# A mixture-of-experts kernel: the first expert product turned round, with the block's matrix as the stationary operand

## Chip, cores and metric

The kernel runs on one core of one Trainium2 chip. The metric is the time of one execution on the device, in microseconds (us), as the median of several runs; the core's engines are called PE (matrix multiplication, with its weight loads shown apart as PEld), DVE (vector), ACT (activation), POOL (general purpose) and SP (which here only issues transfers). All data are fp32, and all products are fp32.

## The reference

Eight sequences of 512 tokens with 256 features go through four steps, each added to the residual: attention with 16 heads and a linear position bias; a mixture of experts; attention with 8 heads and rotary positions; the same mixture of experts again. Both attentions are causal. The mixture of experts, cut to what matters here:

```python
h = x * rsqrt(mean(x * x) + eps) * norm_w          # after a layer norm
logits = h @ gate_w.T + gate_b                     # 8 experts
vals, idx = top_k(logits, 2)
wts = softmax(vals)
t1 = einsum('td,efd->tef', h, mlp1_w) + mlp1_b     # 256 -> 2 x 256
glu = minimum(t1[..., ::2], 7.0)
lin = clip(t1[..., 1::2], -7.0, 7.0)
act = glu * sigmoid(1.702 * glu) * (lin + 1.0)
y = einsum('tei,edi->ted', act, mlp2_w) + mlp2_b   # 256 -> 256
out = x + sum over the two chosen experts of wts * y
```

## The kernel before

**Stages.** An attention stage walks over 8 sequences and 8 head groups; between its steps it puts pieces of other work, among them the norm, gate, choice and count of the experts for the sequence before. When a group of sequences (the first six, then the last two) has been counted, its tokens are sorted by expert into blocks of 128 rows, each block with rows of one expert only: 55 blocks for the first group, 23 for the second, so 78 in each expert stage and 156 in the kernel. Then the expert stage (`run`, lines 960 to 975) works through the blocks. Twice over, this gives: attention, experts, attention, experts.

**One block.** Six steps, each with its own lag behind the block counter `n`, so that several blocks are under way at once:

- `gather` (line 862), four blocks ahead: POOL fetches the block's rows from DRAM by an indirect transfer, four blocks to a tile.
- `turn_rows` (874): PE turns the rows (two transposes into `gtp`), ACT copies them to `hT` (line 882).
- `first` (895), one block later: PE multiplies, with `hT` stationary and the expert's 512 columns moving (line 902), into `hp`, tokens on partitions. DVE adds the bias row (912), caps the gate (913), clips the linear half (916) and multiplies twice (917, 918); ACT computes the sigmoid between them (914). The results lie in one tile `u`.
- `turn_act` (921), three blocks after that: PE turns the result (`atp`, line 927) and ACT copies it to `aT` (929).
- `second` (932): PE multiplies with `aT` stationary (937), DVE adds the second bias (947), POOL scatters the rows to DRAM (948).

All experts' matrices stay in SBUF in one tile `we`. Which expert a block has is known only at run time: `at_block` (885) reads a number into a register of the engine that needs it, and the operand's address is that register plus a constant. The biases lie in a tile `be`, copied to all partitions, so that a block's bias is a row of 512 or 256 columns.

**Order.** PE runs in the order in which the program is written; a scheduler orders the other engines' instructions by its own estimates. [...] Within one iteration of `run`:

```python
at(n + LEAD, self.gather)
at(n - 4, self.turn_act)
at(n, self.turn_rows)
at(n - 1, self.first)
at(n - 4, self.second)
for piece in aside.get(n, ()):
    piece()
```

The `aside` pieces are the rest of the last sequence (about the first eleven iterations), the sorting of the second group (iterations 14, 17 and 20), and, from iteration 60 on, the collecting of finished results: `collect` reads rows back and `add` (line 1018) adds them on DVE to the residual, weighted. In the second expert stage this covers all sequences of the first group, two tiles every other iteration.

**Buffers.** PSUM tiles all come from one ring of eight (`ps`). Of the SBUF rings, `kb` (eight buffers) holds `hT` and `aT`, `S` (four) holds `u`, `V` (two) the results of four blocks, `qk` (two) the gathered rows of four blocks.

**Set-up.** `spread_biases` (192) runs in batch 0: it turns the first bias by PE, sends it to DRAM and reads it back onto all partitions, with 18 transfers in all. `fold_norm` (213) multiplies the norm weights into the gate matrix and the first expert matrices and adds one to the linear half of the bias, on POOL.

Of the kernel before, what the change touches and what calls it, by code (L numbers as in the profile page):

```python
# [35 lines left out]
F32 = mybir.dt.float32  # L36
# [3 lines left out]
ALU = mybir.AluOpType  # L40
# [4 lines left out]
P = 128  # L45
# [30 lines left out]
ROWS = 4  # L76

W_COLS = NC * 2 * FI + FI // P * D
B_COLS = 2 * FI + D

@with_exitstack
def layers(
# [64 lines left out]
    be_sb = const.tile([P, NE * B_COLS], F32, tag="be", name="be")  # L147
    for e in range(NE):
        o = e * W_COLS
        mid = o + NC * 2 * FI  # L150
# [39 lines left out]
    nc.vector.memset(ones, 1.0)  # L190

    def spread_biases():


        b1_sb = work.tile([P, NE * 4], F32, tag="kb", bufs=8, name="b1_p")
        nc.sync.dma_start(out=b1_sb, in_=b1.rearrange("p e m -> p (e m)"))
        b1_ps = ps.tile([NE * 4, P], F32, tag="ps", bufs=8, name="b1_ps")
        nc.tensor.transpose(b1_ps, b1_sb, ident)
        b1_rows = work.tile([NE * 4, P], F32, tag="kb", bufs=8, name="b1_rows")
        nc.vector.tensor_copy(b1_rows, b1_ps)  # L200
        b1_flat = dram.tile([NE * 4, P], F32, tag="b1_flat", name="b1_flat")
        nc.sync.dma_start(out=b1_flat, in_=b1_rows)
        for e in range(NE):
            o = e * B_COLS
            nc.sync.dma_start(
                out=be_sb[:, o : o + 2 * FI],
                in_=b1_flat[4 * e : 4 * e + 4, :].rearrange("m k -> (m k)").partition_broadcast(P),
            )
            nc.sync.dma_start(
                out=be_sb[:, o + 2 * FI : o + B_COLS], in_=b2[e].partition_broadcast(P)  # L210
            )

    def fold_norm():


        for c in range(NC):
            nc.gpsimd.tensor_scalar(
                gates_sb[:, c, 0:NE], gatew_sb[:, c, :], normw_sb[:, c : c + 1], 1.0, ALU.mult, ALU.mult
            )
        for e in range(NE):  # L220
            for c in range(NC):
                w = we_sb[:, e * W_COLS + c * 2 * FI : e * W_COLS + (c + 1) * 2 * FI]
                nc.gpsimd.tensor_scalar(w, w, normw_sb[:, c : c + 1], 1.0, ALU.mult, ALU.mult)
# [297 lines left out]
    class Experts:  # L521


        def __init__(self, kind):
            self.kind = kind
            self.x_mid = dram.tile([NB, T, D], F32, tag=f"x_{kind}", name=f"x_mid_{kind}")
            self.h_all = [
                dram.tile([(hi - lo) * T, D], F32, tag=f"h_{kind}_{i}", name=f"h_all_{kind}_{i}")
                for i, (lo, hi) in enumerate(GROUPS)
            ]  # L530
            self.y_all = [
                dram.tile([2 * PLANE + n * P, D], F32, tag=f"y_{kind}_{i}", name=f"y_{kind}_{i}")
                for i, n in enumerate(BLOCKS)
            ]
# [6 lines left out]
            self.rows, self.hT, self.act, self.ys, self.got = {}, {}, {}, {}, {}  # L541
            self.pairs = {}

        def open_group(self, i):
# [162 lines left out]
        def slots(self, i):  # L707
# [174 lines left out]
            nc.scalar.copy(h, tp)  # L882
            self.hT[i, j] = h

        def at_block(self, i, j, which, engine, cols):
            a = self.R[i]["where"][which]
            return nc.values_load(
                a[0:1, j : j + 1],
                engines=[engine],
                min_val=0,  # L890
                max_val=(NE - 1) * cols,
                skip_runtime_bounds_check_because="the expert's number is clipped",
            )

        def first(self, i, j):
            key = f"{self.kind}_{i}_{j}"
            h = self.hT.pop((i, j))
            wat = self.at_block(i, j, 0, mybir.EngineType.PE, W_COLS)
            bat = self.at_block(i, j, 1, mybir.EngineType.DVE, B_COLS)
            hp = ps.tile([P, 2 * FI], F32, tag="ps", bufs=8, name=f"hp_{key}")  # L900
            for c in range(NC):
                nc.tensor.matmul(  # L902
                    hp,
                    lhsT=h[:, c * P : (c + 1) * P],
                    rhs=we_sb[:, bass.DynSlice(wat + c * 2 * FI, 2 * FI)],
                    start=(c == 0),
                    stop=(c == NC - 1),
                )
            u = work.tile([P, PACKED], F32, tag="S", bufs=4, name=f"u_{key}")
            t, g, a = u[:, 0 : 2 * FI], u[:, 2 * FI : 3 * FI], u[:, 3 * FI : 4 * FI]  # L910
            s = u[:, 4 * FI : 5 * FI]
            nc.vector.tensor_tensor(t, hp, be_sb[:, bass.DynSlice(bat, 2 * FI)], ALU.add)  # L912
            nc.vector.tensor_scalar(g, t[:, 0:FI], LIMIT, 1.0, ALU.min, ALU.mult)  # L913
            nc.scalar.activation(s, g, AF.Sigmoid, scale=ALPHA)  # L914
# [4 lines left out]
            self.act[i, j] = a, wat, bat  # L919

        def turn_act(self, i, j):
            key = f"{self.kind}_{i}_{j}"
            a, wat, bat = self.act.pop((i, j))
            tp = ps.tile([P, FI], F32, tag="ps", bufs=8, name=f"atp_{key}")
            for c in range(FI // P):
                s = slice(c * P, (c + 1) * P)
                nc.tensor.transpose(tp[:, s], a[:, s], ident)  # L927
            aT = work.tile([P, FI], F32, tag="kb", bufs=8, name=f"aT_{key}")
            nc.scalar.copy(aT, tp)  # L929
            self.act[i, j] = aT, wat, bat  # L930

        def second(self, i, j):
            key = f"{self.kind}_{i}_{j}"
            aT, wat, bat = self.act.pop((i, j))
            yp = ps.tile([P, D], F32, tag="ps", bufs=8, name=f"y2_{key}")
            for c in range(FI // P):
                nc.tensor.matmul(  # L937
                    yp,
                    lhsT=aT[:, c * P : (c + 1) * P],
                    rhs=we_sb[:, bass.DynSlice(wat + NC * 2 * FI + c * D, D)],  # L940
                    start=(c == 0),
                    stop=(c == FI // P - 1),
                )
# [12 lines left out]
            tc.declare_no_dep(made.ins, group=group, reason="the rows of the slots differ")  # L956
            tc.add_to_no_dep_group(group, made.ins)
            self.writes[i].append(made.ins)

        def run(self, aside):  # L960
            blocks = [(i, j) for i, n in enumerate(BLOCKS) for j in range(n)]

            def at(n, work_on):
                if 0 <= n < len(blocks):
                    work_on(*blocks[n])

            for n in range(-LEAD, len(blocks) + 4):
# [263 lines left out]
```

## Time and profile before

| | us |
|---|---|
| median of 3 runs (lowest, highest) | 2336.13 (2334.91, 2338.15) |
| profiled execution, its own time | 2302.66 |
| its span, first to last instruction | 2300.8 |
| PE busy | 2229.6 |
| PE weight loads busy | 1452.9 |
| DVE busy | 1635.5 |
| ACT busy | 977.9 |
| POOL busy | 989.9 |
| first product, first and last start, stage one | 937.8 and 1197.7 |
| first product, first and last start, stage two | 2019.6 and 2278.9 |

The durations come from the profiled execution, which was some 33 us shorter than the median of the runs. Busy times are sums of durations. A matmul's end is modelled, and consecutive instructions of one engine overlap in the records, so a busy share is not a rate; where a rate matters it is taken from start to start. In lines of groups the columns are: line, engine, operation, output and inputs, shape, count, then busy us and mean ns of one, then the idle time of the engine just before, and what ended it.

### The profile page before, as it was taken

The page shows a single profiled execution, that of the slowest core. Times are in us where ns is not written, and L with a number is a line of the kernel's source. Part 1 is how long each engine was busy: PE and PEld are TensorE (multiplying, and loading weights), DVE is VectorE, ACT ScalarE, POOL GpSimd, SP SyncE. Part 2 cuts the span into 40 slices and gives each one's busy share as a digit, 9 for nine tenths or more (in the row PEclk, how much of TensorE's full clock was granted, in tenths as well). Part 3 has the DMA queues.
Part 4 walks back from the last instruction along what each step waited for, and adds up shares of the span by engine and source line. Part 5 has one row for each costly group of instructions (what it writes and reads, how often), then busy time and mean ns, then how long its engine had stood idle before and what let it go on. Part 6 is the DMA issues. An engine that isn't in the chain of part 4 may idle for free.

```text
span 2300.8 us, 34673 instructions
## 1 busy us (share of the span) xinstructions
PE 2229.6 (97%) x10657; PEld 1452.9 (63%) x10657; DVE 1635.5 (71%) x4926; ACT 977.9 (43%) x2828; POOL 989.9 (43%) x1374
## 2 busy tenths in 40 slices
PE   8999999999999999899999999999999999999994
PEld 5666666666666666556556666666666666665662
DVE  5566666666666777687877677776867678778787
ACT  4555555555555555323234343443433433433331
POOL 5443434343433343556644333343433434445662
PEclk9999999999999999999999999999999999999997
DMA  7100000000000001222310011010101000022247
GB/s 241 38 28 1 28 1 29 1 28 1 28 1 28 6 28 70 99 79 88 103 52 15 10 37 33 15 46 5 42 10 37 14 33 28 19 78 81 88 156 231
DMA packets 80005, 112.54 MB, mean 49 GB/s; under 512 B 10288, under 2 KB 64720, under 8 KB 79824
## 3 DMA queue, kind: packets, MB, share of 16 engines
q1 hardware_dynamic: 63760, 68.37, 9.0%
q0 software_dynamic: 14976, 40.91, 5.7%
q8 instruction: 89, 1.46, 0.3%
q10 hardware_dynamic: 1088, 1.05, 0.2%
q14 instruction: 92, 0.75, 0.1%
HBM read 68.86 MB, written 41.44 MB: 48 GB/s over the span
## 4 chain that ended last, share of the span: by engine, by line
PE 88%; DVE 7%; issue 2%; POOL 2%; ACT 1%; DMA 1%; DVEq 0%; ACTq 0%; POOLq 0%; SPq 0%
PE pp_a L317 9%; PE pp_b L317 9%; PE hp_f L902 9%; PE op_a L454 6%; PE sp_a L375 6%; PE tp_a L427 6%; PE sp_b L375 6%; PE op_b L454 5%; PE yp_b L472 5%; PE yp_a L472 5%; PE vp_a L298 5%; PE vp_b L298 5%; PE y_f L937 5%; PE tp_b L427 3%; PE atp_f L927 1%
## 5 line engine op out<-in xcount | busy, mean ns | idle before, releaser
L397 ACT ACTIVATE S_a<-S_a,nm_a 128x512 f32<-128x512 f32 (+3 forms) x512 | 280.3, 549 | 306.6 <-DVE nm_a L387 306.5
L330 POOL TENSOR_TENSOR qk_b<-qk_b,rot_b 128x512 f32<-128x512 f32 x128 | 162.8, 1272 | 457.0 <-DVE qk_b L329 446.8
L902 PE MATMUL hp_f<-we,hT_f 128*128 x624 | 294.4, 594 | 0.8 <-ACT hT_f L882 0.8
L356 POOL TENSOR_SCALAR ali_a<-alibi 128x512 f32<-128x512 f32 x128 | 79.4, 620 | 451.0 <-DVE nm_a L387 442.5
L397 ACT ACTIVATE S_b<-S_b,nm_b 128x512 f32<-128x512 f32 (+3 forms) x256 | 142.8, 558 | 235.3 <-DVE nm_b L387 233.8
L387 DVE CUSTOM_DVE_ANT_0 S_a<-sp_a,ali_a 128x512 f32<-128x512 f32 (+3 forms) x512 | 215.9, 486 | 30.7 <-PE sp_a L375 30.5
L412 POOL TENSOR_SCALAR S_a<-S_a,sum_a 128x384 f32<-128x384 f32 (+2 forms) x384 | 205.5, 551 | 34.7 <-DVE sum_a L408 26.2
L948 POOL DMA_INDIRECT y_f<-y_f,row_f x156 | 155.5, 997 | 131.6 <-DVE y_f L947 100.4
L867 POOL DMA_INDIRECT g_f<-h_all_f,token_f x156 | 152.1, 975 | 99.9 <-PE gtp_f L880 58.0
L914 ACT ACTIVATE u_f<-u_f 128x256 f32<-128x256 f32 x156 | 65.1, 417 | 305.0 <-DVE u_f L913 304.8
L937 PEld LDWEIGHTS y_f<-we,aT_f 128*128 128x128 f32 x624 | 117.2, 191 | 110.7 <-issue 53.3
L937 PE MATMUL y_f<-we,aT_f 128*128 x624 | 164.8, 387 | 21.6 <-ACT aT_f L929 21.6
L387 DVE CUSTOM_DVE_ANT_0 S_b<-sp_b,mask 128x512 f32<-128x512 f32 (+3 forms) x256 | 119.1, 484 | 90.5 <-PE sp_b L375 90.5
L375 PE MATMUL sp_b<-qk_b 128*128 128x512 f32 (+3 forms) x512 | 171.9, 438 | 5.0 <-POOL qk_b L330 5.0
L427 PE MATMUL tp_a<-ident,S_a 128*128 128x128 f32 x1280 | 165.3, 276 | 1.1 <-DVE O_a L462 0.6
L427 PEld LDWEIGHTS tp_a<-ident,S_a 128*128 128x128 f32 x1280 | 141.1, 141 | 31.9 <-issue 22.8
L454 PE MATMUL op_a<-PT_a,V_a 128*64 128x384 f32 (+3 forms) x1024 | 154.2, 439 | 3.3 <-ACT PT_a L437 2.2
L912 DVE TENSOR_TENSOR u_f<-hp_f,be 128x512 f32<-128x512 f32 x156 | 107.8, 691 | 68.8 <-PE hp_f L902 61.0
L375 PE MATMUL sp_a<-qk_a 64*128 64x512 f32 (+3 forms) x1024 | 155.5, 443 | 0.9 <-DVE qk_a L334 0.9
L902 PEld LDWEIGHTS hp_f<-we,hT_f 128*128 128x128 f32 x624 | 106.8, 191 | 76.0 <-issue 74.8
L437 ACT COPY PT_a<-tp_a 128x512 f32<-128x512 f32 (+1 forms) x320 | 138.6, 495 | 29.4 <-PE tp_a L427 29.4
L454 PE MATMUL op_b<-PT_b,V_b 128*128 128x512 f32 (+3 forms) x512 | 148.6, 433 | 0.0
(184 smaller groups left out, 4505.6 us busy)
## 6 DMA issues: line engine op xcount, KB each, us to landing
h_all_f<-hn_f SPq DMA_DIRECT2D x64, 128.0 KB, 1.7
xm_f<-x_mid_f SPq DMA_DIRECT2D x16, 512.0 KB, 4.1
yg_f<-y_f SPq DMA_DIRECT2D x64, 128.0 KB, 2.2
yg_f<-y_f SPq DMA_DIRECT2D x28, 256.0 KB, 4.0
x<-x_in_dram SPq DMA_DIRECT2D x8, 512.0 KB, 4.1
we<-w_dram SPq DMA_DIRECT2D x8, 512.0 KB, 7.1
x_mid_f<-x SPq DMA_DIRECT2D x8, 512.0 KB, 2.9
x_mid_f<-xm_f SPq DMA_DIRECT2D x8, 512.0 KB, 3.0
```

Of the source, the lines that this page charges most:

```text
L298: nc.tensor.matmul(vp[:, k, :], lhsT=self.xT[b][:, c, t * P : (t + 1) * P], rhs=wv[:, c, q * 2 * P : (q + 1) * 2 * P], start=(c == 0), sto ...
L317: nc.tensor.matmul(pp, lhsT=w[:, c, g * P : (g + 1) * P], rhs=self.xT[b][:, c, :], start=(c == 0), stop=(c == NC - 1),)
L330: nc.gpsimd.tensor_tensor(qk[:, j, :], qk[:, j, :], rot, ALU.add)
L375: nc.tensor.matmul(sp[i][:, at[it] : at[it] + w], lhsT=qk[r, 0, it * P : (it + 1) * P], rhs=qk[r, 1, 0:w], start=True, stop=True,)
L387: nc.vector.tensor_tensor_reduce(out=s, in0=sp[i][:, at[it] : at[it] + w], in1=add[i][:, T - w : T], scale=scale, scalar=float(np.finfo(np ...
L397: nc.scalar.activation(s, s, AF.Exp, bias=nm[:, it : it + 1], scale=-1.0, accum_out=sums[:, it : it + 1],)
L412: eng.tensor_scalar(s, s, sums[:, it : it + 1], 1.0, ALU.mult, ALU.mult)
L427: nc.tensor.transpose(tp[:, o : o + P], S[:, S_OFF[it] + jt * P : S_OFF[it] + (jt + 1) * P], ident,)
L454: nc.tensor.matmul(op[i * cols : (i + 1) * cols, jt * P : T], lhsT=v[:, jt, c0 : c0 + cols], rhs=PT[i][:, P_OFF[jt] : P_OFF[jt] + T - jt * P],
L472: nc.tensor.matmul(yp[:, 0:D], lhsT=o[:, c, t * P : (t + 1) * P], rhs=wo[:, half * HALF + c, :], start=(c == 0), stop=(c == HALF - 1),)
L902: nc.tensor.matmul(hp, lhsT=h[:, c * P : (c + 1) * P], rhs=we_sb[:, bass.DynSlice(wat + c * 2 * FI, 2 * FI)], start=(c == 0), stop=(c == N ...
L937: nc.tensor.matmul(yp, lhsT=aT[:, c * P : (c + 1) * P], rhs=we_sb[:, bass.DynSlice(wat + NC * 2 * FI + c * D, D)], start=(c == 0), stop=(c ...
```

## The change

The first product is turned round. The block's matrix is stationary and the turned rows move, so that `hp` comes out with the expert's 512 columns on partitions, in four parts of 128, and tokens along the free dimension. The activation then comes out in the layout that the second product wants, and `turn_act` with its copy is gone. Three things follow.

- The 128x1024 part of the expert's matrix is copied on ACT, from its run-time address in `we` to a tile `w1` (ring of three), two blocks ahead (`weights`). PE reads the first product's operands at fixed addresses; only the second product keeps run-time addresses on PE.
- The first bias is now one number per partition: the tile `be` holds eight numbers per expert (gate bias; the lower and the upper limit of the linear half, shifted by the bias; bias plus one; each for two halves). DVE's steps on 512 or 256 columns become steps on 128 columns, each with one or two such numbers as scalar operands at run-time addresses.
- The second bias is copied to all partitions in one transfer into a tile `b2`; the trip of the first bias through PE and DRAM is gone. DVE reads two run-time numbers per block in place of one.

The activation `a` takes a buffer of the `kb` ring. The matrices of `fold_norm` stay as they are.

```diff
-B_COLS = 2 * FI + D
+N_GATE, N_LOW, N_HIGH, N_LIN = 0, 2, 4, 6
+B_COLS = 8
...
+    b1_sb = load(const, [P, NE, 4], b1, "b1")
+    be_sb = const.tile([P, NE, B_COLS], F32, tag="be", name="be")
+    b2_sb = const.tile([P, NE * D], F32, tag="b2", name="b2")
...
     def spread_biases():
...
+        nc.sync.dma_start(
+            out=b2_sb, in_=b2.rearrange("e d -> (e d)").partition_broadcast(P)
+        )
+        lin = b1_sb[:, :, 2:4]
+        nc.gpsimd.tensor_copy(be_sb[:, :, N_GATE : N_GATE + 2], b1_sb[:, :, 0:2])
+        for at, add, by in (
+            (N_LOW, LIMIT, -1.0),
+            (N_HIGH, -LIMIT, -1.0),
+            (N_LIN, 1.0, 1.0),
+        ):
+            nc.gpsimd.tensor_scalar(be_sb[:, :, at : at + 2], lin, add, by, ALU.add, ALU.mult)
...
-            w = be_sb[:, e * B_COLS + FI : e * B_COLS + 2 * FI]
-            nc.gpsimd.tensor_scalar(w, w, 1.0, 1.0, ALU.add, ALU.mult)
...
-            for tag, cols in (("we_at", W_COLS), ("be_at", B_COLS)):
+            for tag, cols in (("we_at", W_COLS), ("be_at", B_COLS), ("b2_at", D)):
...
+        def weights(self, i, j):
+
+            wat = self.at_block(i, j, 0, mybir.EngineType.Activation, (NE - 1) * W_COLS)
+            w = work.tile([P, NC * 2 * FI], F32, tag="w1", bufs=3, name=f"w1_{self.kind}_{i}_{j}")
+            nc.scalar.copy(w, we_sb[:, bass.DynSlice(wat, NC * 2 * FI)])
+            self.w1[i, j] = w
...
         def first(self, i, j):
...
-            for c in range(NC):
-                nc.tensor.matmul(
-                    hp,
-                    lhsT=h[:, c * P : (c + 1) * P],
-                    rhs=we_sb[:, bass.DynSlice(wat + c * 2 * FI, 2 * FI)],
-                    start=(c == 0),
-                    stop=(c == NC - 1),
-                )
+            bat = self.at_block(i, j, 1, mybir.EngineType.DVE, (NE - 1) * B_COLS)
+            dat = self.at_block(i, j, 2, mybir.EngineType.DVE, (NE - 1) * D)
+            hp = ps.tile([P, 4, P], F32, tag="ps", bufs=8, name=f"hp_{key}")
+            for m in range(4):
+                for c in range(NC):
+                    o = c * 2 * FI + m * P
+                    nc.tensor.matmul(
+                        hp[:, m, :],
+                        lhsT=w[:, o : o + P],
+                        rhs=h[:, c * P : (c + 1) * P],
+                        start=(c == 0),
+                        stop=(c == NC - 1),
+                    )
...
-            nc.vector.tensor_tensor(t, hp, be_sb[:, bass.DynSlice(bat, 2 * FI)], ALU.add)
-            nc.vector.tensor_scalar(g, t[:, 0:FI], LIMIT, 1.0, ALU.min, ALU.mult)
+            for m in range(2):
+                nc.vector.tensor_scalar(
+                    half(g, m), hp[:, m, :], number(N_GATE + m), LIMIT, ALU.add, ALU.min
+                )
             nc.scalar.activation(s, g, AF.Sigmoid, scale=ALPHA)
-            lin = t[:, FI : 2 * FI]
-            nc.vector.tensor_scalar(lin, lin, 1.0 - LIMIT, 1.0 + LIMIT, ALU.max, ALU.min)
-            nc.vector.tensor_tensor(g, g, lin, ALU.mult)
+            for m in range(2):
+                nc.vector.tensor_scalar(
+                    half(lin, m),
+                    hp[:, 2 + m, :],
+                    number(N_LOW + m),
+                    number(N_HIGH + m),
+                    ALU.max,
+                    ALU.min,
+                )
+            for m in range(2):
+                nc.vector.scalar_tensor_tensor(
+                    half(g, m), half(lin, m), number(N_LIN + m), half(g, m), ALU.add, ALU.mult
+                )
             nc.vector.tensor_tensor(a, g, s, ALU.mult)
...
-        def turn_act(self, i, j):
...
-            nc.vector.tensor_tensor(y, yp, be_sb[:, bass.DynSlice(bat + 2 * FI, D)], ALU.add)
+            nc.vector.tensor_tensor(y, yp, b2_sb[:, bass.DynSlice(dat, D)], ALU.add)
...
-                at(n - 4, self.turn_act)
+                at(n + 1, self.weights)
```

`number(n)` is one column of `be` at the run-time address plus `n`; `half(t, m)` is 128 columns of a tile.

More of the change, by code (lines that the diff above doesn't have):

```diff
@@ L146, in layers @@
     we_sb = const.tile([P, NE * W_COLS], F32, tag="we", name="we")
-    be_sb = const.tile([P, NE * B_COLS], F32, tag="be", name="be")
+    b1_sb = load(const, [P, NE, 4], b1, "b1")
+    be_sb = const.tile([P, NE, B_COLS], F32, tag="be", name="be")
+    b2_sb = const.tile([P, NE * D], F32, tag="b2", name="b2")
     for e in range(NE):
@@ L192, in spread_biases @@
     def spread_biases():
[L195 to L207, printed above, removed]
-            )
-            nc.sync.dma_start(
-                out=be_sb[:, o + 2 * FI : o + B_COLS], in_=b2[e].partition_broadcast(P)
-            )
+        nc.sync.dma_start(
[9 more added lines that the diff above has]
+            nc.gpsimd.tensor_scalar(be_sb[:, :, at : at + 2], lin, add, by, ALU.add, ALU.mult)
     def fold_norm():
@@ L540, in __init__ @@
             self.hn, self.h, self.both = {}, {}, {}
-            self.rows, self.hT, self.act, self.ys, self.got = {}, {}, {}, {}, {}
+            self.rows, self.hT, self.w1, self.act, self.ys, self.got = {}, {}, {}, {}, {}, {}
             self.pairs = {}
@@ L883, in turn_rows, with at_block @@
             self.hT[i, j] = h
-        def at_block(self, i, j, which, engine, cols):
+        def at_block(self, i, j, which, engine, high):
             a = self.R[i]["where"][which]
@@ L890, in at_block @@
                 min_val=0,
-                max_val=(NE - 1) * cols,
+                max_val=high,
                 skip_runtime_bounds_check_because="the expert's number is clipped",
             )
+        def weights(self, i, j):
[3 more added lines that the diff above has]
+            self.w1[i, j] = w
         def first(self, i, j):
@@ L897, in first @@
             h = self.hT.pop((i, j))
-            wat = self.at_block(i, j, 0, mybir.EngineType.PE, W_COLS)
-            bat = self.at_block(i, j, 1, mybir.EngineType.DVE, B_COLS)
-            hp = ps.tile([P, 2 * FI], F32, tag="ps", bufs=8, name=f"hp_{key}")
-            for c in range(NC):
-                nc.tensor.matmul(
-                    hp,
-                    lhsT=h[:, c * P : (c + 1) * P],
-                    rhs=we_sb[:, bass.DynSlice(wat + c * 2 * FI, 2 * FI)],
-                    start=(c == 0),
-                    stop=(c == NC - 1),
-                )
@@ L909, in first @@
[L909 to L914, printed above, removed]
-            lin = t[:, FI : 2 * FI]
-            nc.vector.tensor_scalar(lin, lin, 1.0 - LIMIT, 1.0 + LIMIT, ALU.max, ALU.min)
@@ L917, in first @@
-            nc.vector.tensor_tensor(g, g, lin, ALU.mult)
-            nc.vector.tensor_tensor(a, g, s, ALU.mult)
-            self.act[i, j] = a, wat, bat
-        def turn_act(self, i, j):
[L922 to L930, printed above, removed]
+            w = self.w1.pop((i, j))
@@ new lines, in first, with number, half @@
+            u = work.tile([P, PACKED], F32, tag="S", bufs=4, name=f"u_{key}")
+            g, lin, s = (u[:, k * FI : (k + 1) * FI] for k in range(3))
+            a = work.tile([P, FI], F32, tag="kb", bufs=8, name=f"a_{key}")
+            flat = be_sb.rearrange("p e n -> p (e n)")
+            def number(n):
+                return flat[:, n : NE * B_COLS][:, bass.DynSlice(bat, 1)]
+            def half(t, m):
+                return t[:, m * P : (m + 1) * P]
+            for m in range(2):
+                nc.vector.tensor_scalar(
+                    half(g, m), hp[:, m, :], number(N_GATE + m), LIMIT, ALU.add, ALU.min
+                )
@@ L932, in second @@
+            nc.vector.tensor_tensor(a, g, s, ALU.mult)
+            self.act[i, j] = a, dat
         def second(self, i, j):
             key = f"{self.kind}_{i}_{j}"
-            aT, wat, bat = self.act.pop((i, j))
+            a, dat = self.act.pop((i, j))
+            wat = self.at_block(i, j, 0, mybir.EngineType.PE, (NE - 1) * W_COLS)
             yp = ps.tile([P, D], F32, tag="ps", bufs=8, name=f"y2_{key}")
             for c in range(FI // P):
+                o = NC * 2 * FI + c * D
                 nc.tensor.matmul(
@@ L938, in second @@
                     yp,
-                    lhsT=aT[:, c * P : (c + 1) * P],
-                    rhs=we_sb[:, bass.DynSlice(wat + NC * 2 * FI + c * D, D)],
+                    lhsT=a[:, c * P : (c + 1) * P],
+                    rhs=we_sb[:, o : NE * W_COLS][:, bass.DynSlice(wat, D)],
                     start=(c == 0),
```

## The prediction

> **What bounds the kernel now.** I read the engine totals first, then the table by stage, the waits of the matmul engine (PE), one block of PE's timeline, and the groups by shape.
>
> ```profile
> PE 2229.6 (97%) x10657; PEld 1452.9 (63%) x10657; DVE 1635.5 (71%) x4926; ACT 977.9 (43%) x2828; POOL 989.9 (43%) x1374
> ...
> 1025.00:1150.00 125.00, 122.94 (x485) 76.75 (x484) 101.66 (x257) 38.10 (x121) 81.00 (x83) 1.00 0.30 95
> ...
> 2107.00:2240.00 133.00, 132.77 (x529) 83.95 (x528) 108.77 (x273) 41.49 (x130) 85.36 (x88) 1.00 0.37 114
> 2240.00:2287.00 47.00, 31.49 (x120) 18.54 (x118) 39.10 (x99) 10.15 (x30) 15.98 (x16) 0.90 0.71 223
> ```
>
> The last three lines are stretches of the two expert stages (start:end, length, then busy us of PE, PEld, DVE, ACT, POOL). In the middle of both, PE is busy nearly throughout; in the last 47 us it is not, and DVE leads. PE's waits and one block:
>
> ```profile
> PE y_f L937 <- ACT aT_f L929: 21.6, 25, 2.4
> ...
> 1150.56 0.38 PE L927 MATMUL atp_f<-ident,u_f 128*128 128x128 f32 x2
> 1150.78 0.38 PE L880 MATMUL gtp_f<-ident,g_f 128*128 128x128 f32 x2
> 1151.00 1.88 PE L902 MATMUL hp_f<-we,hT_f 128*128 x4
> 1152.71 1.03 PE L937 MATMUL y_f<-we,aT_f 128*128 x4
> 1153.58 0.38 PE L927 MATMUL atp_f<-ident,u_f 128*128 128x128 f32 x2
> ```
>
> From start to start a block takes 3.02 us: 0.22 turning the activation, 0.22 turning the rows, 1.71 first product, 0.87 second, with no gap. In the trace's start times, consecutive first-product instructions lie 430 ns apart, second-product ones 216, transposes 109. A busy duration (594 ns for one of hp_f) is longer than its place in the queue, so I price PE by start to start. There are 78 blocks in each of two stages, 156 in all; almost all of the middle ones have this period. The 21.6 us of waits are the only large ones in the expert stages: the copy aT_f stands on ACT behind a sigmoid that waits for a late DVE.
>
> ```profile
> L902 PE MATMUL hp_f<-we,hT_f 128*128 x624 | 294.4, 594 | 0.8 <-ACT hT_f L882 0.8
> L912 DVE TENSOR_TENSOR u_f<-hp_f,be 128x512 f32<-128x512 f32 x156 | 107.8, 691 | 68.8 <-PE hp_f L902 61.0 <-issue 4.2 <-PE gtp_f L880 0.7
> L1018 DVE SCALAR_TENSOR_TENSOR xm_f<-yg_f,wt_f,xm_f 128x256 f32<-128x256 f32 x128 | 68.3, 546 | 9.4 <-DMA yg_f<-y_f 6.4 <-DMA out_dram<-xm_f 1.7
> L914 ACT ACTIVATE u_f<-u_f 128x256 f32<-128x256 f32 x156 | 65.1, 417 | 305.0 <-DVE u_f L913 304.8
> L454 PE MATMUL op_b<-PT_b,V_b 128*128 128x128 f32 x128 | 24.6, 274 | 0.0
> L689 PEld LDWEIGHTS cp_f<-both_f,before 128*128 128x128 f32 x32 | 6.1, 190 | 0.8
> ```
>
> Here the reader sees that DVE now waits for PE at L912 (it has room), and that ACT idles 305 us before its sigmoids.
>
> **What the Trainium skill says.** "TensorE: Matmul & The Clock Gate", LDWEIGHTS (loading the stationary operand): a load takes its columns at 1.2 per ns, 107 ns for 128. The trace agrees: in one run of L689 three loads follow each other after 109 and 113 ns. "VectorE: DVE Perf Modes", Why PSUM operands drop a tier: fp32 from PSUM runs at the single rate; L912 agrees, 608 ns of queue for 512 columns where nothing delays the next. The same page, on the errata: a fixed cost falls on every instruction, so many small tiles pay it often. The trace: L387 from start to the next takes 211, 345, 478, 612 ns for 128 to 512 columns, 77 + 1.045 per column. "ScalarE: Activation LUTs", The pipeline for one element: 0.833 ns per element; L397 on SBUF moves by 0.835.
>
> **The change, part by part** (us against the profiled execution's 2302.66, whose span is 2300.8; the median of the runs shown, 2336.13, is 33 us higher, and I carry the difference over unchanged).
>
> 1. *PE per block.* Gone: two transposes of the activation, 2 x 0.109 = 0.218. The first product goes from 4 instructions at 430 ns (1.72) to 16 of 128 columns with 16 weight loads (four column parts, two halves of the contraction, and fp32 issues each matmul twice, as 624 = 156 x 4 shows). 128-column fp32 pairs exist already: op_b (L454) and sp_b (L375) go 109 to 112 ns from start to start, weight load included. 16 x 0.110 = 1.76. Net -0.218 + 0.04 = -0.178, period 3.02 to 2.84; x 156 = **-27.8**. Bounds: loads at 107 ns give -0.23 (-35), 120 ns give -0.02 (-3). PE's register read moves behind the first product, its queue runs ahead of it, so nothing.
>
> 2. *ACT per block.* Gone: aT_f, 0.25 from start to start. Added: the copy of 128x1024 weights, by the rate above 1024 x 0.835 + 0.04 to 0.18 = 0.9 to 1.04, and a register read of 0.3 (the kind that DVE and PE show), plus the hT_f copy 0.25 and sigmoid 0.32: at most 1.9 of 2.84 us. In the changed program ACT's queue runs sigmoid, hT_f, weights, sigmoid. The sigmoid's input comes when the second product is running, the weights copy by then is over: cost nothing in the middle, because 0.9 us of ACT stay free. Were this cover gone, a late sigmoid would hold DVE's products behind it by up to 1 us. Three weight buffers let the copy run two blocks ahead.
>
> 3. *DVE per block.* Gone, by start to start: L912 0.61 to 0.73, L913 0.21, L916 0.20, two products 0.46 + 0.34; the y add 0.34 stays: 2.15 to 2.27. Added: two gate steps of 128 from PSUM with one scalar operand, two lin steps with two, two products of 128 with one, and a product of 256. The row of L1018 from start to start is 0.396 against 0.335 for the plain product: a scalar operand costs 0.06. So 77 + 134 + 60 = 0.27 for one, 0.33 for two: 2 x 0.27 + 2 x 0.33 + 2 x 0.27 + 0.34 + 0.34 = 2.42. Two register reads instead of one: a read and its address work hold DVE's next instruction 0.48 after the one before (trace, L887 to L912); one lies behind the last product with 0.1 bare. So 2.5; bounds 2.4, and 3.2 when no duration overlaps its successor (eight instructions at full length, 2.9, plus reads 0.3). I take 2.5: 0.34 under PE's 2.84, so off the path in the middle. DVE's room falls from 0.75 to 0.34 per block.
>
> 4. *The waits of 21.6 us.* By stretch: 6.2 and 6.1 at the two stage starts, 4.9 at the end of stage one, 4.4 at the end of stage two. The copy they name is gone. What is late next: hT_f stands behind the sigmoid too, but is wanted a block later, so DVE may lag some 2 us before PE stops, against 0.6 now. Against that DVE catches up more slowly. At the starts normalisation, choice and sorting add some 18 us of DVE work in 24 blocks: 24 x 2.5 + 18 = 78, near PE's own. I take -1 for each start, -4 for the end of stage one (the last four blocks no longer go PE, ACT, PE), 0 for the end of stage two: **-6**, bounds -16 and +8.
>
> 5. *End of stage two.* L1018 adds run there from the 62nd block on. Now two blocks take 6.77 on the chain of waits, through DVE. Then: 2 x 2.5 + 4 x 0.45 = 6.8. So the last 16 blocks keep their time: +16 x 0.178 = **+3** given back, bounds 0 and +10.
>
> 6. *Copies pulled forward.* The changed ACT queue has two weights copies ahead of exponentials of the last attention step, one behind a register read that waits for sorting on DVE. 2 x 1.0 + 0.5 + up to 1.5 of waiting; the exponentials feed POOL's scaling, which has some 3 us before PE turns it: **+2** for both stages, bounds 0 and +8.
>
> 7. *Bias set-up.* Gone: a transpose, a copy, 17 SP transfers and their round trip, eight POOL steps of 0.40; added: one transfer of 16 KB ahead of the weights (0.45 us of SP's issuing), one of 1 MB, four small POOL steps (some 0.27 each) ahead of the scale tables. PE waits for none of it before batch 1; POOL there waits for DVE 0.85. 0, bounds -1 and +2.
>
> POOL keeps its gather and scatter, 1.28 us each from start to start, 2.56 of 2.84; gathers land 13 us ahead, so it stays hidden. Sum: -27.8 - 6 + 3 + 2 = -28.8; I hold back 4 for DVE's bursts on a thinner margin: **-25**, so 2311.
>
> **Rivals.** (a) *DVE becomes the bound between the periods.* At 2.9 to 3.0 us per block the gain is 0.02 to 0.12 x 156 = 3 to 19 less restarts: about 2327. For it: room of only 0.34, eight chained steps, addresses computed before each. Against: the sums above rest on start-to-start times. (b) *Slower: DVE's queue over 3.02 us.* If the added steps do not overlap as those of now do (address work ahead of each, a sigmoid that is late because of the weights copy), 3.2 us gives (3.2 - 3.02) x 156 = +28, less the 3: 2361. It decides from 3.02 us per block. (c) *Weight loads bound the first product.* At 120 ns or more step 1 is gone and waits decide: about 2333. Against: 109 to 113 in three places. (d) The change not doing what it says: the queues show it done; nothing left for this.
>
> **How the numbers follow.** A measurement of this kernel tells about 0.2% (4.7 us) from no change. As forecast 0.61 (2296 to 2327), (a) 0.16, (b) 0.17, (c) 0.06. Faster by over 0.2%: 0.61 + 0.13 + 0.02 = 0.76; within: 0.03 + 0.03 + 0 = 0.06; slower 0.17 + 0.01 = 0.18. The range, 2292 to 2342, takes in the forecast, (a), (c) and the near edge of (b).
>
> **What would show it.** Middle blocks of 2.84 us on PE, 16 first-product starts 110 ns apart; DVE 2.4 to 2.6 per block with waits for PE at the gate steps; weights copies near 1.0 us; waits for aT_f gone. I am wrong if PE waits for the activation or for hT_f in the middle blocks, or if the pairs run at 120 ns or more.

## The result, and the profile after

The changed kernel is slower. Beside the kernel before it took 2397.97 us (median, 2392.6 to 2404.32) against 2337.14; the ratio is 1.0262, 95% interval 1.0235 to 1.0289. Its profiled execution took 2404.32 with a span of 2402.3. The forecast was 2311, and the range ended at 2342.

The engine totals, the groups of the first product, the weights copy and the gate step, then three waits of the changed kernel's profile:

```profile
PE 2252.5 (94%) x12216; PEld 1611.7 (67%) x12216; DVE 1660.1 (69%) x5241; ACT 1088.1 (45%) x2828; POOL 989.8 (41%) x1370
...
L907 PE MATMUL hp_f<-hT_f,w_f 128*128 128x128 f32 x2496 | 336.7, 291 | 84.6 <-ACT hT_f L876 72.4 <-issue 11.9
...
L893 ACT COPY w_f<-we 128x1024 f32 x156 | 163.0, 1046 | 211.3 <-PE hp_f L907 84.9 <-PE gtp_f L874 76.2 <-remote 26.0
...
L926 DVE TENSOR_SCALAR u_f<-hp_f,be 128x128 f32<-128x128 f32 x312 | 96.8, 345 | 136.6 <-PE gtp_f L874 59.5 <-PE hp_f L907 35.6 <-remote 31.0
```

```profile
ACT w_f L893 <- PE hp_f L907: 84.9, 55, 5.4
...
PE hp_f L907 <- ACT hT_f L876: 72.4, 39, 5.1
...
DVE u_f L926 <- PE gtp_f L874: 59.5, 18, 5.1
```

PE now waits for hT_f (72.4 us, up to 5.1 at a time), where it waited 0.8 before; ACT and DVE at the same time wait for PE. Everybody waits for somebody, so the totals alone name no culprit. Nor are the prices of single instructions far off: the copy takes 1046 ns, first-product pairs start 112 ns apart, and an undisturbed block takes 2.87 us. But such blocks come in runs of a few, and between them blocks take some 3.5 to 7. The same two stretches of the expert stages as before (start:end, length, then busy us of PE, PEld, DVE, ACT, POOL, and the granted clock) show it:

```profile
1025.00:1150.00 125.00, 105.02 (x710) 94.53 (x709) 82.54 (x264) 54.13 (x99) 65.08 (x66) 0.93 0.23 68
2107.00:2240.00 133.00, 109.70 (x772) 99.73 (x772) 93.56 (x329) 57.91 (x104) 66.30 (x67) 0.95 0.22 68
```

PE, all but saturated before, lacks some 20 us in each. (On the clock of these views the first products of the kernel before start from 926.6 to 1186.6 and from 2008.5 to 2267.8 us; the four starts in the table of its times are given some 11.1 us later.) One disturbance in the timeline of the changed kernel (start, duration, engine and line, idle time before it and who ended it):

```profile
1107.09 1.95 PE L907 MATMUL hp_f<-hT_f,w_f 128*128 128x128 f32 x16
1107.21 0.95 POOL L861 DMA_INDIRECT g_f<-h_all_f,token_f  x1 [0.30 <-issue]
...
1108.46 0.99 POOL L964 DMA_INDIRECT y_f<-y_f,row_f  x1 [0.30 <-DVE u_f L940]
...
1109.76 0.96 POOL L861 DMA_INDIRECT g_f<-h_all_f,token_f  x1 [0.30 <-issue]
1109.96 1.95 PE L907 MATMUL hp_f<-hT_f,w_f 128*128 128x128 f32 x16
1111.03 0.99 POOL L964 DMA_INDIRECT y_f<-y_f,row_f  x1 [0.30 <-issue]
...
1113.27 0.61 DVE L926 TENSOR_SCALAR u_f<-hp_f,be 128x128 f32<-128x128 f32 x2 [4.22 <-PE hp_f L907]
1113.32 1.05 ACT L893 COPY w_f<-we 128x1024 f32 x1 [5.44 <-PE hp_f L907]
...
1115.00 0.38 PE L907 MATMUL hp_f<-hT_f,w_f 128*128 128x128 f32 x1 [1.20 <-ACT hT_f L876]
```

By its record the product of 1107.09 is over at 1109.04, but the DVE step that reads it starts at 1113.27, and the copy on ACT starts at the same moment. In the trace PE's semaphore, which both wait for, is not raised from 1107.42 to 1113.24, then six times within 0.6 us. DVE's own semaphore was raised at 1108.28 and 1109.06 in the same gap, at once after its steps, so it is not that every engine's semaphore stood still. PE's reports of finished work came some 4 us late, and PE's own wait for hT_f at 1115.00 is only the echo. A matmul's end is modelled: whether the products or only their reports were late, the trace cannot say. "Report" below means the raising of that semaphore. POOL meanwhile issues indirect transfers 1.25 to 1.4 us apart; the reports came 1.2 us after the end of the last one.

### The profile page after: what moved, and what is told of

It is laid out like the page before. It is cut to its first block, busy times and chain, and to the rows that moved or that the text cites. A ratio compares the mean times of both kernels' runs of the same rounds, so it can differ in the third digit from the quotient of the medians.

```text
span 2402.3 us, 38747 instructions
## 1 busy us (share of the span) xinstructions
PE 2252.5 (94%) x12216; PEld 1611.7 (67%) x12216; DVE 1660.1 (69%) x5241; ACT 1088.1 (45%) x2828; POOL 989.8 (41%) x1370
## 4 chain that ended last, share of the span: by engine, by line
PE 86%; DVE 6%; issue 2%; ACT 2%; POOL 1%; DMA 1%; another core or an unknown queue 1%; DVEq 0%; ACTq 0%; SPq 0%; POOLq 0%
PE hp_f L907 11%; PE pp_a L311 9%; PE pp_b L311 9%; PE op_a L448 6%; PE sp_a L369 6%; PE tp_a L421 6%; PE sp_b L369 6%; PE op_b L448 5%; PE yp_b L466 5%; PE yp_a L466 5%; PE vp_a L292 5%; PE y_f L953 4%; PE vp_b L292 4%; PE tp_b L421 3%; PE gtp_f L874 2%
## 5 line engine op out<-in xcount | busy, mean ns | idle before, releaser
L907 PE MATMUL hp_f<-hT_f,w_f 128*128 128x128 f32 x2496 | 336.7, 291 | 84.6 <-ACT hT_f L876 72.4
L907 PEld LDWEIGHTS hp_f<-hT_f,w_f 128*128 128x128 f32 x2496 | 315.8, 205 | 98.5 <-ACT hT_f L876 82.4
L893 ACT COPY w_f<-we 128x1024 f32 x156 | 163.0, 1046 | 211.3 <-PE hp_f L907 84.9
L926 DVE TENSOR_SCALAR u_f<-hp_f,be 128x128 f32<-128x128 f32 x312 | 96.8, 345 | 136.6 <-PE gtp_f L874 59.5
L953 PE MATMUL y_f<-we,a_f 128*128 x624 | 172.0, 398 | 9.5 <-issue 5.4
L448 PEld LDWEIGHTS op_a<-PT_a,V_a 128*64 128x64 f32 x1024 | 70.7, 137 | 100.6 <-issue 70.1
```

The lines of the kernel that those rows point to most:

```text
L448: nc.tensor.matmul(op[i * cols : (i + 1) * cols, jt * P : T], lhsT=v[:, jt, c0 : c0 + cols], rhs=PT[i][:, P_OFF[jt] : P_OFF[jt] + T - jt * P],
L893: nc.scalar.copy(w, we_sb[:, bass.DynSlice(wat, NC * 2 * FI)])
L907: nc.tensor.matmul(hp[:, m, :], lhsT=w[:, o : o + P], rhs=h[:, c * P : (c + 1) * P], start=(c == 0), stop=(c == NC - 1),)
L953: nc.tensor.matmul(yp, lhsT=a[:, c * P : (c + 1) * P], rhs=we_sb[:, o : NE * W_COLS][:, bass.DynSlice(wat, D)], start=(c == 0), stop=(c == ...
```

## The experiments

Each group of runs has its own runs of the kernel before; each ratio is to these. "Long gaps" are stretches over 3.9 us without a report of PE that begin between 1005 and 1180 or between 2110 and 2270 us of the run's trace; the silence after the last block of a stage is not counted. They are only the longest stalls. "Lost" is therefore given beside them: the time from the 21st to the 61st block of both stages, by the starts of the first product in the same trace, less 80 blocks of the length that the run's undisturbed blocks have (2.87 us in the changed kernel, 3.02 in the one before, 2.81 in e2, 3.03 in h2, 3.09 in e1 and f8).

| Kernel | us | ratio (95%) | long gaps | lost, us |
| --- | --- | --- | --- | --- |
| changed kernel | 2397.97 | 1.0262 (1.0235 to 1.0289) | 24 | 77 |
| e1: before, 16 pairs | 2425.75 | 1.0345 (1.0322 to 1.0368) | 18 | 92 |
| e2: changed, 8 wide pairs | 2371.08 | 1.0111 (1.0089 to 1.0132) | 20 | 59 |
| e3: changed, no weights copy | 2392.06 | 1.0200 (1.0177 to 1.0224) | 26 | 71 |
| e4: changed, no PE register read | 2410.87 | 1.0283 (1.0261 to 1.0304) | 26 | 71 |
| e5: changed, no gathers on POOL | 2289.68 | 0.9745 (0.9724 to 0.9766) | 1 | 0 |
| e6: before, no gathers on POOL | 2297.90 | 0.9784 (0.9764 to 0.9804) | 0 | 0 |
| e7: changed, single-row buffers | 2344.93 | 0.9986 (0.9974 to 0.9997) | 26 | 37 |
| e8: before, two blocks to a buffer | 2313.17 | 0.9848 (0.9826 to 0.9870) | 1 | 5 |
| f1: before, second profile | 2341.61 | | 8 | 31 |
| f2: changed, two blocks to a buffer | 2342.97 | 0.9994 (0.9983 to 1.0005) | 12 | 27 |
| f4: changed, POOL busy, no gathers | 2293.72 | 0.9792 (0.9776 to 0.9808) | 2 | 0 |
| f8: changed, PE slower on purpose | 2410.29 | 1.0291 (1.0274 to 1.0308) | 20 | 64 |
| h1: changed, again | 2414.20 | 1.0290 (1.0272 to 1.0307) | 20 | 80 |
| h2: before, 8 pairs | 2370.08 | 1.0097 (1.0076 to 1.0119) | 3 | 54 |
| h3: before, two blocks, again | 2313.11 | 0.9863 (0.9838 to 0.9888) | 1 | 4 |

In these groups the kernel before took 2337 to 2348. In one more group it took 2303.93; its three kernels (g1, g7, g8) are told apart from the rest. Where the record names the chip of a group, it is 10 for e1 to e4, 9 for e5 to e8, 1 for the f and h runs, and 4 for that one group alone, so whether the chip or the time makes the difference cannot be told.

**Which part of the change: the short pairs, the copy, or the register read.** e1 does one part alone:

```diff
-            for c in range(NC):
-                nc.tensor.matmul(hp, lhsT=h[:, c * P : (c + 1) * P], rhs=we_sb[:, bass.DynSlice(wat + c * 2 * FI, 2 * FI)], ...)
+            for m in range(4):
+                for c in range(NC):
+                    o = c * 2 * FI + m * P
+                    nc.tensor.matmul(hp[:, m * P : (m + 1) * P], lhsT=h[:, c * P : (c + 1) * P], rhs=we_sb[:, o : o + P], ...)
```

> The kernel before with one edit: the first product is issued as 16 short pairs of weight load and matmul (128 columns each) in place of 4 long ones (512 columns); for fixed operands it always reads the matrix of expert 0, so the routing of that product is left out. Tokens stay on partitions, the activation is still turned, DVE, ACT and the waits are those of before. Theory A (PE's load of short instructions: the changed kernel issued 18 PE instructions per us where the kernel before issued 11, and PE's reports of finished work came up to 6 us late): the same disturbance appears here, blocks of 3.0 us broken by stalls of several us, time 2380 to 2410. Theory B (ACT's queue: the weights copy waits for PE ahead of hT on ACT, and PE waits for hT): there is no copy here, so blocks stay near 3.05 us and the time near that of before, 2325 to 2345. Theory C (the register read of the second product on PE): nothing changes, as in B.

e2 keeps everything but the number of pairs (`for m in range(2)`, `rhs=h`, output `hp[:, 2 * m : 2 * m + 2, :]`):

> The changed kernel with one edit: the first product is issued as 8 pairs of 256 columns (both halves of hT as moving operand at once) in place of 16 pairs of 128, with the same time on PE (8 x 216 = 1.73 us against 16 x 110 = 1.76); half of the stationary blocks are left out, so hp is not the product of the reference. Copy, register reads, ACT, DVE and all waits stay. Theory A: PE issues some 12.5 instructions per us, the stalls go, blocks of 2.84 us, time 2300 to 2320. Theories B and C: the stalls stay, 2385 to 2410.

e3 takes `w = we_sb[:, 0 : NC * 2 * FI]` and drops `weights`:

> The changed kernel without the weights copy on ACT: the first product always reads the matrix of expert 0 at a fixed address, so its routing is left out. ACT keeps the sigmoid and hT alone. Theory A: stalls stay, 2385 to 2410. Theory B: stalls go, 2300 to 2320. Theory C: stays, 2385 to 2410.

e4 takes `rhs=we_sb[:, o : o + D]` in `second` and drops its register read:

> The changed kernel without the register read on PE: the second product always reads the matrix of expert 0 at a fixed address, so its routing is left out; per block a TENSOR_LOAD of 0.3 us, two register operations and a semaphore instruction leave PE's queue. Theory A: 4 to 6 of some 52 instructions per block less, so most of the stalls stay, 2360 to 2400. Theory B: stays, 2385 to 2410. Theory C: the stalls go, 2300 to 2320.

The pairs alone, in the kernel before, cost 3.45%, more than the whole change; 2425.75 lies above theory A's 2380 to 2410. Without the copy the changed kernel still lost 2.0%, without the register read 2.83%: theories B and C fall, the copy being a smaller part at most. Half as many pairs left 1.1%, so theory A held in part only: it wanted the stalls gone, and 20 long gaps remained, with 59 us lost where the changed kernel lost 77. The regular stalls of e1 show what A lacked. Timeline of e1:

```profile
1110.28 0.98 POOL L867 DMA_INDIRECT g_f<-h_all_f,token_f  x1 [2.78 <-PE gtp_f L880]
...
1111.56 0.98 POOL L950 DMA_INDIRECT y_f<-y_f,row_f  x1 [0.31 <-DVE u_f L920]
...
1112.85 1.05 POOL L867 DMA_INDIRECT g_f<-h_all_f,token_f  x1 [0.30 <-issue]
1112.93 1.95 PE L904 MATMUL hp_f<-we,hT_f 128*128 128x128 f32 x16
...
1114.20 0.96 POOL L867 DMA_INDIRECT g_f<-h_all_f,token_f  x1 [0.30 <-issue]
...
1115.47 0.95 POOL L867 DMA_INDIRECT g_f<-h_all_f,token_f  x1 [0.30 <-issue]
...
1116.72 0.99 POOL L950 DMA_INDIRECT y_f<-y_f,row_f  x1 [0.30 <-issue]
1118.93 0.69 DVE L914 TENSOR_TENSOR u_f<-hp_f,be 128x512 f32<-128x512 f32 x1 [4.65 <-PE hp_f L904]
```

POOL waits for PE to free a row buffer, then issues six indirect transfers, 1.25 to 1.35 us apart. With the third transfer of the train, its second gather (the text of e5 below says the third), PE's reports stop (at 1113.11); they come back 1.19 us after its last instruction has ended. All 18 long gaps of e1 end 1.1 to 1.4 us after the last indirect transfer. The trains come from the buffers: four blocks share one, so POOL's queue has four gathers and four scatters for every four blocks.

**POOL's indirect transfers.** Theory D is that PE's reports stay out while POOL issues such trains. e5 and e6 make the same edit in the changed kernel and in the one before:

```diff
-            nc.gpsimd.indirect_dma_start(out=self.rows[i, j // ROWS][:, j % ROWS, :], ..., in_offset=bass.IndirectOffsetOnAxis(...))
+            at = (j % 8) * P
+            nc.sync.dma_start(out=self.rows[i, j // ROWS][:, j % ROWS, :], in_=self.h_all[i][at : at + P, :])
```

> The changed kernel with the gathers taken off POOL: the rows of each block come by a plain DMA from SP of 128 rows in a row, so the choice of rows by the routing is left out. PE, ACT, DVE and POOL's scatters stay. Theory D: PE's reports of finished work stay out while POOL issues indirect DMAs back to back (in the kernel with 16 pairs every stall began at the third of four gathers in a row and ended 1.1 to 1.4 us after POOL's last DMA instruction), so with one indirect DMA per block the stalls go: 2285 to 2315. Theory E (PE alone: it stalls by its own rate of short instructions, POOL only shows the same rhythm because its row buffers are freed by PE): the stalls stay, 2385 to 2410.

> The kernel before with the gathers taken off POOL in the same way (rows by a plain DMA from SP, the choice of rows left out). The profiled execution before ran its middle blocks at a flat 3.02 us, so theories D and E both expect no more than the waits for aT to change: 2325 to 2345; if the time of the unprofiled runs holds stalls of theory D that the profile didn't show, it falls to 2300 to 2315.

f4 adds to e5, in `second`, `nc.gpsimd.tensor_tensor(pad, y[:, 0:NT], mhalf, ALU.pow)`:

> The changed kernel without gathers on POOL (rows by a plain DMA from SP, the choice of rows left out), and in their place a small computing instruction of POOL of about the same length in each block (a power of 128x4 numbers, some 1.0 us, its result unused). If it is the indirect DMAs that hold PE's reports back (theory D), no stalls: 2285 to 2315. If it is POOL being busy, whatever it does, or scatters that come late (theory G), the stalls return: over 2340.

Theory D held, E and G fell: the same PE work without gathers on POOL took 2289.68, and POOL kept busy with computing 2293.72; neither lost anything in the 80 blocks. The same stretches of e5:

```profile
1025.00:1150.00 125.00, 124.99 (x959) 118.19 (x959) 112.03 (x354) 70.43 (x130) 40.81 (x43) 1.00 0.32 100
2107.00:2240.00 133.00, 129.54 (x986) 121.73 (x985) 120.01 (x377) 73.53 (x134) 42.95 (x45) 1.00 0.41 130
```

PE is busy throughout, with 959 matmuls in 125 us where the changed kernel ran 710. What nobody had expected is e6: the kernel before, whose profile showed no stall, also gained 2.2%. f1 is the kernel before, profiled once more.

> The kernel before once more, for its profile. Its first profiled execution took 2302.7 us, 33 less than the median of the runs; without gathers on POOL it ran 2297.9. Theory D (PE's reports stay out while POOL issues indirect DMAs back to back): a second profile shows stalls of this kind in the middle blocks and 2320 to 2350, so that the first was a fortunate one. Theory F (the profiler's own effect makes this kernel faster): flat blocks of 3.02 us again, 2300 to 2306.

```profile
1025.00:1150.00 125.00, 113.85 (x440) 69.31 (x440) 87.06 (x221) 36.26 (x111) 73.01 (x75) 1.00 0.27 80
```

PE 113.85 us in the stretch in place of 122.94: eight long gaps, 2341.61 us. The profile that the prediction was worked from was of an execution without stalls.

Two limits of theory D. Trains alone are not enough: that first profile has 18 trains of six or more transfers (starts less than 1.5 us apart) in the stretches of the table, f1's has 23, and yet in the first PE is never silent for more than 1.95 us. And the edit of e5 and e6 changes several things at once: who issues the transfer, on which queue it runs, and the order of the rows. The traces do not separate POOL's issuing from the transfers that it starts: in e1 the last packet of a train ends between 0.34 us before and 0.45 us after the reports come back.

**The trains broken up, with the whole computation.** e7 and f2 in the changed kernel, e8 and h3 in the one before; e8 and f2 are

```diff
-            if j % ROWS == 0:
-                self.rows[i, j // ROWS] = work.tile([P, ROWS, D], F32, tag="qk", ...)
+            if j % 2 == 0:
+                self.rows[i, j // 2] = work.tile([P, 2, D], F32, tag="qk", ...)
```

and e7 has a ring `g1` of seven `[P, D]` tiles, with `w1` cut to two.

> The changed kernel with a row buffer of its own for each block (a ring of seven tiles of 128x256) in place of four blocks to a buffer; the ring of weights copies is cut from three to two to make room. Nothing of the computation is left out. POOL's order is then gather, scatter, gather, scatter in place of four gathers and four scatters, so no train of gathers forms. Theory D: the stalls go or shrink to a quarter, 2290 to 2330. Theory E: they stay, 2385 to 2410. A ring of two for the weights may cost up to 0.2 us per block by itself (30 us), which would show as waits for w.

> The changed kernel with two blocks to a row buffer in place of four, the ring of weights copies at three as it was: POOL's order is gathers and scatters in pairs at most. Nothing of the computation is left out. Theory D: as with single rows or better, 2320 to 2350, since POOL still has 2.57 us of indirect DMAs in a block of 2.87 us. Theory E (PE's own rate): 2385 to 2410.

> The kernel before with two blocks to a row buffer in place of four, so that POOL's order is gather and scatter in turn. Nothing of the computation is left out. Theory D: no change in a kernel that shows no stalls (2330 to 2345), or a gain of up to 30 us if the unprofiled runs hold some. Theory E: no change. Gathers that come only three blocks ahead may cost up to 10 us.

In the kernel before this one edit is worth 1.5% (again 1.4% in h3): **2313 us, the best version with the whole computation** in groups where the kernel before takes 2345 to 2348, and a little more than the 30 us that theory D allowed. In the changed kernel breaking up the trains brings 2.6 to 3.0% (0.9986 or 0.9994 over 1.0262 to 1.0290) and so just the time of the unedited kernel before. POOL there has two transfers, 2.57 us, in a block of 2.87, and trains of up to five still form when it catches up. f2 came out as theory D expected; e7 did not: 2344.93 is above its 2290 to 2330, and its long gaps did not become fewer (26), though the loss halved (37 us in place of 77). f8 tests whether POOL's free time is all (the loop over `nc.tensor.transpose` in `turn_rows` stands twice):

> The changed kernel with PE made slower on purpose: the two transposes of each block's rows are done twice, 0.22 us more on PE in each of 156 blocks, so an undisturbed block takes 3.09 us, and POOL, with its 2.57 us of indirect DMAs per block, has 0.52 us free in place of 0.30. Same results. If the stalls come from POOL's share of the block (theory D with a threshold in POOL's free time), they go and the kernel gets faster in spite of the added work: 2325 to 2350. If they come from the short pairs of PE whatever POOL's share: 34 us slower than the changed kernel, 2420 to 2445.

Neither came true: 2410.29, within the 2398 to 2414 of the changed kernel. A block of 3.09 us, longer than before's 3.02, stalls all the same and loses twice as much (64 us against f1's 31), so POOL's share of the block alone does not decide. PE's added work vanished in the stalls: in the 80 blocks it is 17 us (80 x 0.22), and f8 lost 16 less than h1, which ran on the same chip.

**How many pairs, and the group without stalls.** g1, g7 and g8 ran in the group where the kernel before took 2303.93. g1 writes each block's rows with `nc.sync.dma_start` to rows in order.

> The kernel before with the first product in 8 pairs of 256 columns in place of 4 of 512 (the matrix of expert 0 at a fixed address, its routing left out; 8 x 216 = 1.73 us of PE against 4 x 430 = 1.72). With 4 pairs the kernel took 2337 to 2345, with 16 pairs of 128 columns 2426. If the stalls grow with the number of short pairs: between these, 2360 to 2400. If only pairs as short as their own weight load matter: 2335 to 2350.

> The kernel before with the first product in 16 pairs of 128 columns (expert 0 at a fixed address) and with the gathers taken off POOL (rows by a plain DMA from SP, their choice left out): the fourth corner beside 4 pairs with gathers (2337 to 2345), 4 pairs without (2298) and 16 pairs with (2426). If short pairs cost nothing by themselves and only together with POOL's two indirect DMAs per block: 2290 to 2310. If they cost by themselves: over 2350.

> The changed kernel with the scatters taken off POOL in place of the gathers: each block's products are written by a plain DMA from SP to rows in a row, so the placing by the routing is left out; the gathers stay on POOL, in fours, each first of four waiting for PE to free the row buffer. If two indirect DMAs per block are too many whichever they are: stalls go, 2285 to 2315. If it is the gathers, four in a row behind a wait for PE: stalls stay at 2340 or more.

g7 took 2306.35 (ratio 1.0006, interval 0.9999 to 1.0013) and g8 2306.39 (1.0008, 1.0000 to 1.0017): where nothing stalls, 8 pairs with gathers and 16 without cost within 0.2% of 4. g1 took 2294.62 (0.9956, 0.9939 to 0.9972) with one long gap, behind the last first product of stage two; since I have no run of the changed kernel itself in that group, it does not tell whether taking the scatters away would do what taking the gathers away does. The last group, with the kernel before at 2345.13:

> The changed kernel once more beside the kernel before. In the last group of runs the kernel before took 2304, as its first profile showed, where in all earlier groups it took 2337 to 2348: whether its stalls appear differs from one group of runs to another. If this group is like the last (before at 2304): theory D with stalls that depend on the session gives either 2290 to 2300 for the changed kernel (no stalls at all, as without gathers) or something above 2340 (short pairs still bring them on). If it is like the earlier ones (before at 2340 to 2348): 2395 to 2410.

> The kernel before with the first product in 8 pairs of 256 columns, once more (expert 0's matrix at a fixed address, its routing left out). In a group where the kernel before takes 2340 or more: between it and the 16 pairs, 2360 to 2400, if the stalls grow with the number of pairs; 2335 to 2350 if only the shortest pairs matter. In a group with the kernel before at 2304: 2306 again.

> The kernel before with two blocks to a row buffer, once more. In a group where the kernel before takes 2340 or more: ratio 0.985 as before. In a group with the kernel before at 2304: little left to gain, 2300 to 2312, perhaps some us slower since gathers come only three blocks ahead.

With 4, 8 and 16 pairs the kernel before took 2345, 2370 and 2426: the loss grows with the number of pairs (0, 1.0, 3.5%), as in the changed orientation (1.1% with 8 wide, 2.6 to 2.9% with 16). h2 stalls in shorter gaps: it has three long ones and lost 54 us.

**What stays open.** Why many short pairs make PE's reports so sensitive to POOL's trains, and whether it is the issuing or the transfers; the trace shows no common resource. One possibility that fits is named by the Trainium skill, "DMA: Bandwidth & Descriptors", Terms: transfers issued by POOL have their descriptors written to rings in SBUF; no run here shows that PE is held up there. Open too is why one group of runs, and the first profile, had no stalls; whether the changed kernel would have been free of them there was not seen. PE's instruction fetches do not fit as a cause: in e1's trace they come anywhere from 6.1 us before the start of a long gap to 4.0 us after it, and some gaps have none so near.

## Why the prediction was wrong, step by step

The edit was priced against the wrong background, and too well even without it. Without the gathers on POOL the changed kernel took 2289.68 and the one before 2297.90: a gain of 8.2, where 25 were forecast. With them the changed kernel lost 69 (h1: 2414.2 - 2345.1). So the gathers on POOL cost the changed kernel 2414.2 - 2289.7 = 124.5 us and the kernel before 2345.1 - 2297.9 = 47.2. The difference, 77, is the price that I missed; the other 17 us of the error are a smaller gain. The times are from different groups, whose kernels before differ by 3 us, and the 77 is a subtraction, not a measurement of its own.

- **The step that failed** is the sentence on POOL: "gathers land 13 us ahead, so it stays hidden". It asked only whether the data come in time. No wait of PE for them shows in the changed profile; what costs is that the gathers run on POOL's queue at all, through PE's reports. Why they do so stays open. None of the rivals had it. Rival (b) had the sign, and its 2361 was neither the size nor the mechanism: in the undisturbed blocks DVE fits (step 3).
- **The base.** "I carry the difference over unchanged": the 33 us between the profiled execution (2302.66) and the median (2336.13) fit stalls of the kind that f1's profile shows; the timed runs of that group have no trace. They were the one visible sign that something in the timed runs was missing from the page, and that something grew with the edit.
- **Step 1**, -27.8: pairs at 112 ns, not 110, make the block 2.87 where 2.84 was forecast, -0.15 x 156 = -23. The pairs did not go at 120 ns; rival (c) is out.
- **Step 2**: 1046 ns for the copy, against 0.9 to 1.04 us; the 0.833 ns per element stands in the Trainium skill, "ScalarE: Activation LUTs", Step-by-step: what each stage is for, and 1024 of them leave 0.19 us for the fixed part, where 0.04 to 0.18 had been taken. It hides in e5, where no block of the middle is longer than 2.87 us; e3 lies 0.6 to 0.9% below the changed kernel, which is all that it could be worth in the stalling kernel.
- **Step 3**: in an undisturbed block of e5, DVE's steps by start times are 2 x 0.26 (gate), 2 x 0.32 (linear), 0.27 + 0.46 (products, the second with a register read behind it), 0.34 and 0.33: 2.56 against 2.5. Some 0.25 of waiting for the sigmoid comes on top, so DVE just fits.
- **Step 4**, -6: in e5 the waits for aT_f (21.6) are gone, but PE waits 24.7 us for hT_f in their place:

```profile
PE hp_f L906 <- ACT hT_f L875: 24.7, 17, 3.4
```

 Of these, 18.7 us lie at the two stage starts, where the waits for aT_f were 6.2 and 6.1. The note that hT_f "stands behind the sigmoid too" was right, the credit was not.
- **Steps 4 to 6 by stretches**: from the first to the 21st block e5 takes 85.1 us and e6 79.5 in stage one, 81.3 and 79.7 in stage two, so the starts cost 7 us. Steps 1 and 4 had together made them some 9 shorter: nearly all of the 17 us went here. Besides the waits for hT_f, e5 has four spells of half clock in these stretches and e6 one. From the 21st to the 61st it is 114.8 against 120.8 in both stages, the saving of step 1. The last 17 blocks of stage one take 55.5 against 58.5, which is no more than step 1; those of stage two take 54.2 against 54.4, so they keep their time, as step 5 said. Sum of both stages: 505.7 against 513.6, the 8 us. Of the +2 of step 6 nothing shows before the first product (928.4 us in e5, 928.7 in e6).
- **Step 7**, at 0, fits the same two starts. PE's register read, also priced at nothing: e4 took it out and gained nothing.

The half clock in the changed profile (0.93 and 0.95 in the stretches above) is no cause of its own. One such spell of the changed kernel, with the stretches around it:

```profile
1090.30:1096.80 6.50, 5.00 (x33) 3.84 (x31) 1.39 (x5) 0.37 (x1) 4.10 (x5) 1.00 0.34 105
1097.35:1104.18 6.83, 5.64 (x22) 5.17 (x23) 6.13 (x21) 4.12 (x8) 1.94 (x2) 0.50 0.11 38
1104.20:1107.40 3.20, 3.20 (x27) 3.05 (x26) 2.30 (x8) 1.51 (x3) 2.13 (x3) 1.00 0.14 41
```

In the first stretch, a stall, PE runs dry; in the second it gets half the clock and pairs start 213 ns apart. The Trainium skill, "TensorE: Matmul & The Clock Gate", Part 1, says that an idle window of some 3.4 us takes the clock to half. The spells here last 3.4 or 6.8 us, which agrees; but PE was not wholly idle before this one, with 1.40 us busy in the 3.41 ahead of it. It lengthens a stall, it does not start one: in f1 the stalls come at a clock of 1.00.

## What to carry to other kernels

When the timed runs are longer than the profiled execution by ten times their own spread, find what the page does not show before pricing an edit on it: take a second profile. An engine that only issues transfers belongs in the sum with its rhythm, not only with its lead: where indirect transfers cost anything here, trains of six and seven went with 77 and 80 us lost in 80 blocks of the changed kernel, trains of up to five with 27 and 37, and the edit of the row buffers was worth more than the change under study. Splitting a long matmul into short pairs is not always free just because the array time is equal: beside POOL's gathers it cost up to 3.5%, without stalls nothing over 0.2%.

## What I had not expected of the hardware

- PE's semaphore stayed unraised for 4 to 9 us while POOL issued indirect transfers 1.25 to 1.4 us apart, and then came up to six times within 0.6 us; during the first 3 us or so PE's matmul starts went on at their normal 112 ns.
- The same kernel, unedited, took 2304 in one group of runs, the only one on its chip, and 2337 to 2348 in the others.
- With equal array time (1.72 to 1.79 us per block), 4, 8 and 16 pairs gave 2345, 2370 and 2426 us.
